# A two-layer graph convolution on one core: blocks of 256 nodes in layer 1, five PSUM banks in layer 2's list

## The chip, the cores and the metric

The kernel runs on one core of a Trainium2 chip. The metric is the time of one execution on the device, in microseconds (us). Before the change it is 3094.66 us, the median of 3 runs (3094.16 to 3096.91). The engines are named as the profile names them: PE (TensorE: matmuls and transposes), DVE (VectorE), ACT (ScalarE), POOL (GpSimd, which issues the gathers) and SP (SyncE, which issues most other transfers).

## The reference, cut to what matters

There are 12500 nodes with 128 features, 200000 edges sorted by their destination, and ten relations. The relation of an edge is the argmax of ten of its 42 attributes.

```python
def _rgcn_layer(x, src, dst, edge_type, w_rel, root, bias):
    N = x.shape[0]
    seg = dst * NUM_REL + edge_type
    xs = x[src]
    sums = jax.ops.segment_sum(xs, seg, num_segments=N * NUM_REL)
    cnt = jax.ops.segment_sum(jnp.ones(seg.shape, x.dtype), seg, num_segments=N * NUM_REL)
    mean = (sums / jnp.maximum(cnt, 1.0)[:, None]).reshape(N, NUM_REL, -1)
    return jnp.einsum('nrd,rdo->no', mean, w_rel) + x @ root + bias
...
edge_type = jnp.argmax(msg[:, NODE_EMB_DIM:-NODE_EMB_DIM], axis=1).astype(jnp.int32)
h = jax.nn.relu(_rgcn_layer(x, src, dst, edge_type, w_rel1, root1, b1))
return _rgcn_layer(h, src, dst, edge_type, w_rel2, root2, b2)
...
x = _layernorm(x + _L0_gnn_ref(...), axis=-1)
```

Each layer gathers the source's row for each edge, averages the rows for each pair of destination and relation, multiplies by the relation's matrix, and adds the node's own row times `root` and a bias. Layer 2 needs `h`, the result of layer 1, of the edge's source, which can be any node.

## The kernel before, in words

**Tiles and bunches.** The edges are cut into 1563 tiles of 128 (`NT`); four tiles (`QB`) are a bunch. For a tile POOL gathers the sources' rows (`gathered`, L747 to 750). DVE writes a one-hot matrix, edge against relation and node, with up to 12 neighbouring nodes (`ones`, L757). ACT scales it by one over the edge's count (`weighted`, L752). PE multiplies the gathered rows by it into a PSUM bank (`zp`, L976 in layer 1, L1479 in layer 2), and DVE adds the product at the tile's place to a ring of 1024 nodes and ten relations in SBUF (`cc`; `sum_into`, L781 to 790). There are two such rings. The order of the instructions on each engine is written out by hand: `layer_1` and `layer_2` are loops over bunches, and the classes `Later` (L792) and its `job` put further work at a tile's number.

**Both layers in one pass.** When all tiles of a block of nodes have been added, `finish` (L838) projects the block. Ten matmuls read the ring, an eleventh adds the `root` part (`projected`, L730, with L737 and L740), ACT evacuates with bias and ReLU (`shifted`, L665), PE turns the block over, ACT copies it (`rows_kept`, L861), and SP stores the rows of `h` to DRAM. They go to `hD` and, for the blocks up to `K1`, to two tables `XH` with rows of 256 numbers: a node's `x` and, once it is ready, its `h` (zero before). From tile 166 (`T0`) on, a gather from `XH` takes both halves, so a tile serves layer 1 and, for sources that are ready, also layer 2: the second matmul of a tile at L976, into the second ring. The block's layer-2 ring is projected in the same way (`second`), and its sum goes to `T2` in DRAM. The rings are then cleared by ACT (`cleared`, L715).

**Epochs.** Which rows of `h` a gather sees must be known when the program is built. The tiles from `T0` on are grouped in 127 rows of 11 tiles (1408 edges). An epoch (L116 to 123) begins with the first row that starts at least `READY` = 6 bunches after a block's `finish`. The gathers of an epoch read one of the two tables, those of the next epoch the other one (`table_of`, L126). A block is stored into the one table as soon as it is ready and into the other one when the epoch that reads that one has ended (`todo_late`, L867 to 873). A table's gather waits for the stores into it, a store waits for the gathers before it.

**The list of layer 2.** Edges whose source was not yet ready, and all edges of the first 166 tiles, are left for `layer_2`. Lines 131 to 181 work out from the share of nodes still missing, with 4.25 deviations of room, how many slots each row needs; in sum 709 tiles of 128 slots (`NT2`). On the chip, `brought_together` (L1057) compacts the 127 rows into this list while the 166 plain tiles are gathered from `hD`: mask (`seen_below`, `rooms`, filled by `row_limits`, L386), prefix sums, a shifting network of eleven steps on DVE, then `listed` (L1218) for the indices, keys, weights and offsets of 128 tiles at a time. `tile_limits` (L404) fills the limits of the offsets.

**Layer 2's loop** (L1450 to 1515) runs over bunches of one or more tiles that fill one PSUM bank. `ones` runs `AH` = 4 bunches ahead of the product, the addition to the ring `BE` = 2 bunches behind it, the products take the three buffers of `ps_y`. Gathers go eight to a buffer, with seven buffers (`GB`). For nodes that spread over more than 48 columns a tile has several bunches, each with its own table of columns (`tables[c, WZ]`, L1169 to 1173, in three banks of PSUM, `mask`). `finish` (L1391) projects a block of 256 nodes, adds `T2`, norms it (`normed`, L691) and stores the output. Its follow-up steps come some tiles later, or at once when all gathers are issued (`u`, L1397).

**Blocks of layer 1.** `starts` (L84): 23 blocks of 512 nodes (`YB`), then six of 128 or less, so 29 calls of `finish`. `KSEEN` = (1, 21) gives 21 epochs.

```python
    starts = list(range(0, N - YB - 2 * P, YB))
    starts += list(range(starts[-1] + YB, N, P))
```

Of the kernel before, what the change touches and what calls it, by code (L numbers as in the profile page):

```python
# [9 lines left out]
F32 = mybir.dt.float32  # L10
# [10 lines left out]
P = 128  # L21
NREL = 10
# [26 lines left out]
KSEEN = (1, 21)  # L49
# [14 lines left out]
def rgcn_resnorm_kernel(ctx: ExitStack, tc: tile.TileContext, x, src, dst, attr, w_rel1, root1, b1,  # L64
# [19 lines left out]
    starts = list(range(0, N - YB - 2 * P, YB))  # L84
    starts += list(range(starts[-1] + YB, N, P))
# [264 lines left out]
    def places():  # L350
# [5 lines left out]
        for size in (YB, P):  # L356
            for k in range(NBLK - 1):
                if done_after(k) < NT and starts[k + 1] - starts[k] == size:
                    early(0, nc.vector.scalar_tensor_tensor(lows, even, STEP * done_after(k) - 0.5, lows,
                                                            op0=ALU.is_gt, op1=ALU.add))  # L360
            if size == YB:
                early(0, nc.vector.tensor_scalar(lows, lows, float(YB // P), None, op0=ALU.mult))
# [310 lines left out]
    def block_rows(a, k, l):  # L673
# [83 lines left out]
    def ones(keys, cols, n, w):  # L757
# [7 lines left out]
        else:  # L765
            nc.vector.tensor_tensor(o.rearrange("p (t r n) -> p t r n", r=NREL, n=w),  # L766
                                    cols[:, None, :, :w].to_broadcast([P, n, NREL, w]),
                                    keys[:, :, None, None].to_broadcast([P, n, NREL, w]), op=ALU.is_equal)
# [61 lines left out]
    def layer_1():  # L830
# [5 lines left out]
        big = [k for k in range(NBLK) if block(k)[1] == YB]  # L836

        def finish(k, t):  # L838
# [22 lines left out]
            def rows_kept(_):  # L861
                pr = po.pop()
                hb = fin.tile([P, 4, C], F32, name="hb")
# [34 lines left out]
            if both:  # L898
                w = 10 if k >= NBLK - 3 else 6
                todo.at(t + w * u, lambda t: cleared(1, k, 0))  # L900
                todo.at(t + (w + 1) * u, lambda t: cleared(1, k, 1))
            if k + 1 < NBLK - 1:
# [16 lines left out]
                w = 2 if k == NBLK - 3 else 5  # L919
# [113 lines left out]
    row_limits()  # L1033
# [23 lines left out]
    def brought_together(ready, first):  # L1057
# [116 lines left out]
        assert WMAX * NREL <= ER  # L1174
# [5 lines left out]
        def put(i, c):  # L1180
# [5 lines left out]
            o = WMAX * NREL + i * (EW // P)  # L1186
# [101 lines left out]
    def layer_2():  # L1288
# [155 lines left out]
        AH, BE = 4, 2  # L1444
# [5 lines left out]
        for p in range(-AH, NB + BE):  # L1450
            if p + AH < NB:
# [3 lines left out]
                ohs[p + AH] = ones(keys[:, t0:t0 + n], tables[(c, WZ) if second else WN], n, w)  # L1455
# [32 lines left out]
            q = p - BE  # L1488
            if q >= 0:
# [199 lines left out]
```

## Time and profile before

| | |
|---|---|
| median of 3 runs | 3094.66 us (3094.16 to 3096.91) |
| profiled execution | 3098.4 us, its span 3096.6 us |
| busy of the span: PE, DVE, ACT, POOL | 78%, 64%, 42%, 75% |
| mean granted PE clock | 0.823 of full speed |
| moved by DMA | 371.57 MB, 120 GB/s in the mean |
| gathers (POOL) | 166 from `x`, 1397 from `XH`, 166 from `hD` for the plain tiles, 709 from `hD` for the list |

How to read it: the span runs from the first to the last instruction of one profiled execution. A line such as `L749 POOL DMA_INDIRECT g<-XH,idxE x1397` is a group: source line, engine, operation, what it writes and reads, and how many. In a timeline each row begins with the start, then the duration; in brackets stands how long the engine had been idle before and what released it. "Issue" is time in which the engine waited for nothing that the profile shows. In a row of stretches each engine has its busy time and its number of instructions, in the order PE, PE's weight loads, DVE, ACT, POOL, followed by the granted clock, the DMA share and GB/s; a row for one engine has that engine's alone. A row of waits has the total, the number and the longest. A group's row by source line has the durations as least/median/greatest in ns and the first and last start in us. Float32 matmuls appear as two records each.

### The profile page before, as it was taken

What the parts mean: (1) busy time and instruction counts of PE and PEld (TensorE: products, weight loads), DVE (VectorE), ACT (ScalarE), POOL (GpSimd) and SP (SyncE); (2) the same over time, 40 slices, a digit from 0 to 9 for tenths busy, and PEclk for the clock granted to TensorE, in tenths of its full rate; (3) what the DMA queues carried; (4) which work ended last, traced back from release to release, by engine and by line L of the source; (5) the groups of instructions that cost most, each with busy time, mean ns of one, the idle gap of its engine ahead of it and who ended that gap; (6) DMA issues with size and microseconds to landing.
All of it is one profiled execution on the core that took longest, in us unless ns stands there. A gap on an engine that the chain in (4) does not pass through costs nothing.

```text
span 3096.6 us, 39943 instructions
## 1 busy us (share of the span) xinstructions
PE 2427.0 (78%) x10905; PEld 1805.4 (58%) x10905; DVE 1989.1 (64%) x5272; ACT 1292.9 (42%) x3006; POOL 2308.9 (75%) x2450
## 2 busy tenths in 40 slices
PE   2768887888888888888888899646577787777887
PEld 2546666566666566666666667545555555555665
DVE  7875746465656565555555554598677677677676
ACT  3543333333333333333333334322445555555453
POOL 7777777777777777777777777677777777777774
PEclk8768888888888878787888789856788999988888
DMA  7865445454545454545454444322222222222222
GB/s 210 233 204 173 143 124 159 120 163 123 163 119 163 121 162 124 162 123 162 123 161 124 127 121 120 101 58 63 60 70 74 73 74 74 74 74 73 74 73 59
DMA packets 260631, 371.57 MB, mean 120 GB/s; under 512 B 49654, under 2 KB 189467, under 8 KB 260404
## 3 DMA queue, kind: packets, MB, share of 16 engines
q0 software_dynamic: 100368, 251.49, 29.5%
q1 hardware_dynamic: 106339, 91.83, 9.6%
q10 hardware_dynamic: 53697, 25.62, 2.8%
q8 instruction: 94, 1.54, 0.2%
q14 instruction: 133, 1.09, 0.1%
HBM read 323.78 MB, written 57.76 MB: 123 GB/s over the span
## 4 chain that ended last, share of the span: by engine, by line
PE 37%; POOL 18%; issue 16%; DVE 13%; DMA 11%; ACT 3%; DVEq 1%; ACTq 0%; POOLq 0%; SPq 0%
POOL g L749 18%; PE pf L737 16%; DMA g<-XH,idxE 10%; PE zp L976 9%; PE zp L1479 8%; DVE cc L790 4%; DVE oh L766 2%; PE pf L740 1%; ACT cc L720 1%; ACT oh L755 1%; DVE cc L1157 1%; PE pf L1195 1%; DVEq L775 1%; DVE oh L763 1%; DVE go L1145 1%
## 5 line engine op out<-in xcount | busy, mean ns | idle before, releaser
L749 POOL DMA_INDIRECT g<-XH,idxE x1397 | 1321.7, 946 | 425.6 <-issue 383.9
L790 DVE TENSOR_TENSOR cc<-cc,zp 128x240 f32 (+16 forms) x2507 | 962.9, 384 | 719.7 <-PE zp L976 503.1
L976 PE MATMUL zp<-oh,g 128*128 128x120 f32 x5920 | 1053.4, 334 | 323.6 <-DMA g<-XH,idxE 230.5
L976 PEld LDWEIGHTS zp<-oh,g 128*128 128x128 f32 x5920 | 926.1, 236 | 482.4 <-issue 187.1
L749 POOL DMA_INDIRECT g<-hD,idxB x709 | 670.2, 945 | 216.1 <-issue 202.7
L755 ACT ACTIVATE oh<-oh,wE 128x120 f32<-128x120 f32 x1729 | 530.2, 383 | 640.8 <-DVE oh L763 557.3
L1479 PE MATMUL zp<-oh,g 128*128 128x120 f32 (+18 forms) x1888 | 514.8, 417 | 256.8 <-DVE cc L790 102.3
L737 PE MATMUL pf<-cc,w 128*128 128x256 f32 (+6 forms) x2120 | 691.4, 485 | 30.3 <-DVE cc L790 21.3
L1479 PEld LDWEIGHTS zp<-oh,g 128*128 128x128 f32 x1888 | 346.1, 230 | 401.8 <-issue 252.2
L737 PEld LDWEIGHTS pf<-cc,w 128*128 128x128 f32 x2120 | 411.8, 208 | 279.6 <-issue 205.0
L755 ACT ACTIVATE oh<-oh,wB 128x150 f32<-128x150 f32 (+18 forms) x778 | 342.6, 483 | 293.7 <-DVE oh L766 276.6
L766 DVE TENSOR_TENSOR oh<-go,keyB 128x480 f32<-128x480 f32 (+14 forms) x478 | 262.9, 550 | 132.8 <-PE zp L1479 131.6
L720 ACT ACTIVATE cc<-zero 128x2560 f32<-128x2560 f32 (+4 forms) x188 | 322.0, 1717 | 21.7 <-DVE cc L790 19.6
L763 DVE TENSOR_TENSOR oh<-bank,keyE 128x480 f32<-128x480 f32 x391 | 253.2, 648 | 0.0
L670 ACT ACTIVATE a<-pf,b 128x512 f32<-128x512 f32 (+1 forms) x27 | 17.3, 639 | 453.6 <-PE pf L740 453.6
L749 POOL DMA_INDIRECT g<-hD,idxE x166 | 158.4, 954 | 62.6 <-issue 46.6
L749 POOL DMA_INDIRECT g<-in_x_dram,idxE x166 | 157.0, 946 | 52.3 <-issue 47.2
L546 DVE TENSOR_TENSOR eqb<-bank,kh 128x1344 bf16<-128x1344 f32 (+2 forms) x65 | 100.5, 1549 | 2.3 <-PE pf L557 1.9
L555 PE MATMUL pf<-eqb,identb 128*128 128x512 bf16 (+2 forms) x130 | 64.7, 498 | 11.6 <-DVE eqb L546 11.4
L882 ACT ACTIVATE v<-pf,b 128x512 f32<-128x512 f32 (+2 forms) x29 | 18.0, 619 | 120.1 <-PE pf L740 100.5
L557 PE MATMUL pf<-eqb,identb 128*128 128x512 bf16 (+2 forms) x130 | 64.1, 493 | 0.0
L415 DVE SCALAR_TENSOR_TENSOR reach<-u,reach 128x6 f32<-128x6 f32 x252 | 42.2, 167 | 7.4
(235 smaller groups left out, 991.5 us busy)
## 6 DMA issues: line engine op xcount, KB each, us to landing
m<-in_edge_attr_dram SPq DMA_DIRECT2D x48, 672.0 KB
g<-XH,idxE POOLq DMA_INDIRECT x1397
XH<-in_x_dram ACTq DMA_DIRECT2D x24, 512.0 KB
XH<-zero ACTq DMA_DIRECT2D x24, 512.0 KB
g<-hD,idxB POOLq DMA_INDIRECT x709
XH<-hb SPq DMA_DIRECT2D x43, 256.0 KB
out_dram<-o SPq DMA_DIRECT2D x47, 128.0 KB
xb<-in_x_dram SPq DMA_DIRECT2D x23, 256.0 KB
```

The lines of the kernel that those rows point to most:

```text
L546: nc.vector.tensor_tensor(eq[:p], kpP[:p, None, :R].to_broadcast([p, DB, R]), fore, op=ALU.is_equal)
L555: nc.tensor.matmul(pc[:p], identb[:p, :p], eq[:p, k:k + 4, L:], start=(d + k == 1), stop=False)
L557: nc.tensor.matmul(pc[:p], identb[:p, :p], back, start=False, stop=(d + k + 3 == L))
L720: nc.scalar.activation(cc[:, l, h * H:(h + 1) * H, o:o + n], zero[:, None, :n].to_broadcast([P, H, n]), AF.Copy)
L737: nc.tensor.matmul(po[:, :n], wsb[l][:, r, :], cc[:, l if ring is None else ring, r, o:o + n], start=(r == 0), stop=False)
L749: nc.gpsimd.indirect_dma_start(out=g[:, j * C:(j + n) * C], out_offset=None, in_=table, in_offset=bass.IndirectOffsetOnAxis(ap=idx, axis=0))
L755: nc.scalar.activation(s, s, AF.Copy, scale=w)
L763: nc.vector.tensor_tensor(o.rearrange("p (t m) -> p t m", m=m), cols[:, None, :m].to_broadcast([P, n, m]), keys[:, :, None].to_broadcast([ ...
L766: nc.vector.tensor_tensor(o.rearrange("p (t r n) -> p t r n", r=NREL, n=w), cols[:, None, :, :w].to_broadcast([P, n, NREL, w]), keys[:, :, ...
L790: nc.vector.tensor_tensor(s, s, z, op=ALU.add)
L976: nc.tensor.matmul(zp[:, a + l * KW:a + (l + 1) * KW], g[:, (slot[j] + l) * C:(slot[j] + l + 1) * C], oh[:, j * KW:(j + 1) * KW], start=Tr ...
L1479: nc.tensor.matmul(zp[:, j * m:(j + 1) * m], gt[:, b * C:(b + 1) * C], oh[:, j * m:(j + 1) * m], start=True, stop=True)
```

## The change

- Layer 1's large blocks have 256 nodes (`BN`), so `finish` is called 52 times. `KSEEN` = (3, 43) covers the same nodes and gives 41 epochs. `hb`, the copy that is stored, has two buffers of half the size; some follow-up steps of `finish` come one bunch sooner.
- `row_limits` is no longer run before layer 1. It is a job from bunch 180 on, one step every two bunches; `tile_limits` moves from bunch 8 to bunch 80.
- The tables `XH` are filled piece by piece in one rhythm (the first piece of the second table comes second), and the last piece at bunch 38 instead of 51.
- Layer 2 keeps one table of 48 columns; for later columns `ones` adds the shift `c` to it. The two banks of `mask` that this frees take products: in five bunches three use `ps_y` and two these banks, once the list is built. From then on additions run three bunches behind (`BE` = 3).

```diff
-KSEEN = (1, 21)
+BN = 2 * P
+KSEEN = (3, 43)
...
-    starts = list(range(0, N - YB - 2 * P, YB))
-    starts += list(range(starts[-1] + YB, N, P))
+    starts = list(range(0, N - YB - 2 * P, BN))
+    starts += list(range(starts[-1] + BN, N, P))
...
-        for size in (YB, P):
+        for size in (BN, P):
...
             was_k, was = starts[k + 1], now
+            yield 1
...
-    def ones(keys, cols, n, w):
+    def ones(keys, cols, n, w, c=0):
...
+            to = o.rearrange("p (t r n) -> p t r n", r=NREL, n=w)
+            a = cols[:, None, :, :w].to_broadcast([P, n, NREL, w])
+            b = keys[:, :, None, None].to_broadcast([P, n, NREL, w])
+            if c:
+                assert n == 1
+                nc.vector.scalar_tensor_tensor(to[:, 0], a[:, 0], float(c), b[:, 0], op0=ALU.add, op1=ALU.is_equal)
+            else:
+                nc.vector.tensor_tensor(to, a, b, op=ALU.is_equal)
...
-                hb = fin.tile([P, 4, C], F32, name="hb")
+                hb = fin.tile([P, 2, C], F32, name=f"hb{k % 2}")
...
-                        assert k <= K0 or t >= first_seen[k - 1]
+                        assert k <= K0 or now + QB >= first_seen[k - 1]
...
-                todo.at(t + (9 if k >= NBLK - 3 else 5) * u, second_kept)
+                todo.at(t + (9 if k >= NBLK - 3 else 4) * u, second_kept)
...
-                w = 10 if k >= NBLK - 3 else 6
+                w = 10 if k >= NBLK - 3 else 5
...
-                w = 2 if k == NBLK - 3 else 5
+                w = 2 if k == NBLK - 3 else 4
...
-        jobs.job(8 * QB, tile_limits(), 2 * QB)
-        for b in range(2):
-            for i, a in enumerate(range(0, N, 2 * YB)):
-                n = i + b * 13
-                jobs.at((1 + n * 3 // 2 if n < 22 else 1 + n * 2) * QB, lambda t, b=b, a=a: table_rows(b, a))
+        jobs.job(80 * QB, tile_limits(), 2 * QB)
+        jobs.job(180 * QB, row_limits(), 2 * QB)
+        pieces = [(b, a) for b in range(2) for a in range(0, N, 2 * YB)]
+        pieces.insert(1, pieces.pop(len(pieces) // 2))
+        for n, (b, a) in enumerate(pieces):
+            jobs.at((1 + n * 3 // 2) * QB, lambda t, b=b, a=a: table_rows(b, a))
...
     places()
-    row_limits()
...
-        for c in range(0, WMAX, WZ):
-            w = min(WZ, WMAX - c)
-            t = mask[:, c * NREL:(c + w) * NREL].bitcast(F32).rearrange("p (r n) -> p r n", n=w)
-            nc.vector.tensor_scalar(t, wide[:, :, :w], float(c), None, op0=ALU.add)
-            tables[c, WZ] = t
+        tables[WZ] = mask[:, :WZ * NREL].bitcast(F32).rearrange("p (r n) -> p r n", n=WZ)
+        nc.vector.tensor_copy(tables[WZ], wide)
...
-        AH, BE = 4, 2
+        AH, BE = 4, 3
+        plain = sum(not b[1] for b in bunches)
...
+            five = p >= plain and "ring" in ready
...
-                zp = zps[p] = ps_y.tile([P, YB], F32, name="zp")
+                if p % 5 > 2 and five:
+                    b = p % 5 - 2
+                    zp = mask[:, b * YB:(b + 1) * YB].bitcast(F32)
+                else:
+                    zp = ps_y.tile([P, YB], F32, name="zp")
+                zps[p] = zp
...
-            q = p - BE
-            if q >= 0:
+            q = p - (BE if five else BE - 1)
+            if q in zps:
```

More of the change, by code (lines that the diff above doesn't have):

```diff
@@ L360, in places @@
                                                             op0=ALU.is_gt, op1=ALU.add))
-            if size == YB:
-                early(0, nc.vector.tensor_scalar(lows, lows, float(YB // P), None, op0=ALU.mult))
+            if size == BN:
+                early(0, nc.vector.tensor_scalar(lows, lows, float(BN // P), None, op0=ALU.mult))
         early(0, nc.vector.tensor_scalar(lows, lows, float(P), None, op0=ALU.mult))
@@ L835, in layer_1 @@
         offs, row = None, None
-        big = [k for k in range(NBLK) if block(k)[1] == YB]
         def finish(k, t):
@@ L859, in rows_out, with rows_kept @@
                 po.append(pr)
-            def rows_kept(_):
+            def rows_kept(now):
                 pr = po.pop()
-                hb = fin.tile([P, 4, C], F32, name="hb")
+                hb = fin.tile([P, 2, C], F32, name=f"hb{k % 2}")
                 for p, s in spans(k):
@@ L1168, in brought_together @@
         yield 1
-        for c in range(0, WMAX, WZ):
-            w = min(WZ, WMAX - c)
-            t = mask[:, c * NREL:(c + w) * NREL].bitcast(F32).rearrange("p (r n) -> p r n", n=w)
-            nc.vector.tensor_scalar(t, wide[:, :, :w], float(c), None, op0=ALU.add)
-            tables[c, WZ] = t
-        assert WMAX * NREL <= ER
+        assert WZ * NREL <= YB
+        tables[WZ] = mask[:, :WZ * NREL].bitcast(F32).rearrange("p (r n) -> p r n", n=WZ)
+        nc.vector.tensor_copy(tables[WZ], wide)
         n = -(-NT2 // P)
@@ L1185, in put @@
             assert m * P <= EW
-            o = WMAX * NREL + i * (EW // P)
+            o = WZ * NREL + i * (EW // P)
             assert o + EW // P <= EW - KW
@@ L1454, in layer_2 @@
                 assert not second or {t0 // P, (t0 + n - 1) // P} <= ready
-                ohs[p + AH] = ones(keys[:, t0:t0 + n], tables[(c, WZ) if second else WN], n, w)
+                ohs[p + AH] = ones(keys[:, t0:t0 + n], tables[WZ if second else WN], n, w, c)
             if 0 <= p + AH - 1 < NB:
```

3 lines of the change are left out of this document (removed).

## The prediction

> **What bounds the kernel now.** The page comes first: the span, the busy times and the chain that ended last.
>
> ```profile
> span 3096.6 us, 39943 instructions
> PE 2427.0 (78%) x10905; PEld 1805.4 (58%) x10905; DVE 1989.1 (64%) x5272; ACT 1292.9 (42%) x3006; POOL 2308.9 (75%) x2450
> PE 37%; POOL 18%; issue 16%; DVE 13%; DMA 11%; ACT 3%; DVEq 1%; ACTq 0%; POOLq 0%; SPq 0%
> ```
>
> Both of the last rows point at PE, with 78% busy and 37% of the chain. That is misleading. A chain followed back from the end can run through PE because PE is waiting for a gather, and a busy share says nothing about who sets the pace. So the second view is the one source line that all of POOL's gathers have (L749): its durations, first and last starts, and what POOL waited for before them.
>
> ```profile
> L749 POOL DMA_INDIRECT g<-XH,idxE x1397: 942/946/1139, 211.8 to 1957.8; - x200
> L749 POOL DMA_INDIRECT g<-hD,idxB x709: 940/944/1436, 2180.1 to 3065.2; - x178
> L749 POOL DMA_INDIRECT g<-in_x_dram,idxE x166: 940/944/1107, 4.1 to 210.5; - x166
> L749 POOL DMA_INDIRECT g<-hD,idxE x166: 940/944/1842, 1971.1 to 2178.8; - x166
>   issue: 680.4, 2233
>   PE zp L976: 28.6, 94
>   DMA hD<-hb: 12.4, 1
> ```
>
> 2233 of the 2438 gathers waited for nothing but their own issue, 0.30 us each. The 94 that stand under PE also waited 0.30 us each (28.6/94), so PE happened to end in that gap and held up nobody. One wait is real, 12.4 us for the last rows of layer 1. The timeline of POOL gives the ends of the two stretches.
>
> ```profile
> 4.15 1.11 POOL L749 DMA_INDIRECT g<-in_x_dram,idxE  x1 [1.98 <-DVE lane L333]
> 1957.81 0.95 POOL L749 DMA_INDIRECT g<-XH,idxE  x1 [0.30 <-issue]
> 1971.11 0.94 POOL L749 DMA_INDIRECT g<-hD,idxE  x1 [12.35 <-DMA hD<-hb]
> 3065.15 0.94 POOL L749 DMA_INDIRECT g<-hD,idxB  x1 [0.30 <-issue]
> ```
>
> Layer 1 has 166+1397 = 1563 gathers, and (1957.81-4.15)/1562 = 1.2507 us from start to start. Layer 2 has 166+709 = 875, and (3065.15-1971.11)/874 = 1.2518 us. A gather with its issue takes 0.945+0.30 = 1.245 us, so POOL loses under 0.01 us per gather in either layer. **POOL's gather rate is the bound everywhere.** The span is 4.15 + 1953.66 + 13.30 (hand-over between the layers) + 1094.04 + 31.45 (last gather's start to the end) = 3096.6 us. The profiled execution took 3098.4 us, 1.8 more than its span, and 3.7 more than the median of the runs, 3094.66.
>
> **The change part by part.** Only what alters the number of gathers, one of the three margins, or POOL's pace can move the time.
>
> *The list of layer 2.* Each row of the list (11 tiles, 1408 edges; 127 rows) keeps the edges whose source lies past the last block of layer 1 that was ready. With blocks of 256 a new limit comes after 2 or 3 rows instead of 5 or 6. Worked through the planner's lines 116 to 181 with both settings, 59 rows have a limit that is 256 nodes higher. That is 256/12500 x 1408 = 28.8 edges fewer in each, 1701 edges or 13.3 tiles of 128. With the allowances and rounding the list falls from 709 tiles (the x709 above) to 695. The plain gathers stay 1563 and 166. So 14 gathers go, 14 x 1.2518 = **-17.5 us**. The count is fixed when the program is built, so no data can take it back.
>
> *Layer 1's finishes, 29 become 52.* PE has 40 us per 256 nodes (32 tiles x 1.25).
>
> ```profile
> 1248.23 8.76 PE L737 MATMUL pf<-cc,w 128*128 128x512 f32 x20
> 2606.46 5.81 PE L737 MATMUL pf<-cc,w 128*128 128x256 f32 x20
> 3040.72 4.48 PE L737 MATMUL pf<-cc,w 128*128 128x256 f32 x20
> 925.81 3.73 PE L976 MATMUL zp<-oh,g 128*128 128x120 f32 x32
> 800.00:1200.00 400.00, 341.21 (x1603) 249.40 (x1601) 233.11 (x530) 153.56 (x364) 302.50 (x321) 0.82 0.48 141
> ```
>
> The tiles' own products take 8 x 16 records x 3.73/32 = 14.9 us of the 40 when PE catches up. The two projections took 8.76 per 256 nodes (half of 2 x 8.76) and will take 2 x 4.48 to 2 x 5.81, so PE needs 23.7 us now and 23.9 to 26.5 then. PE's 341 busy us of 400 become at most 341 + 10 x 2.9 = 370 (10 half-blocks in 400 us): still no bound. PE reaches the gathers' pace again after every finish, and a burst is 5 us long instead of 9. I take **0**. ACT's clears stay the same area, and its evacuations are 23 sets more, beside 153.56 busy of 400.
>
> *Limits and tables on DVE.* `row_limits` had 20 steps of 8 small instructions ahead of layer 1; now 40 steps run from bunch 180 on. `places` gets 23 instructions more.
>
> ```profile
> L383 DVE TENSOR_SCALAR some<-place x86: 83/146/154, 8.9 to 345.3; 128x1 f32<-128x1 f32 x86
> L384 DVE TENSOR_TENSOR rooms<-rooms,some x60: 92/151/221, 10.2 to 84.9; 128x1 f32<-128x1 f32 x60
> L359 DVE SCALAR_TENSOR_TENSOR lows<-even,lows x28: 269/278/280, 44.0 to 54.2; 13x128 f32<-13x128 f32 x28
> 45.00:70.00 25.00, 18.90 (x21) 0.58 0.74 226
> 120.00:145.00 25.00, 18.91 (x21) 0.91 0.60 167
> ```
>
> The old steps (80 pairs of L383 and L384) ran from 9 to 85 us, and POOL's gathers kept their length beside them: 18.90 us for the gathers in 45 to 70 us, 18.91 in 120 to 145 us, after the steps had ended. So the early part loses 160 x 0.15 = 24 us of DVE work and gains 23 x 0.278 = 6.4 us, and neither was on the path. Later, 320 x 0.15 = 48 us lie between tiles 720 and 1040 (about 900 to 1300 us), where DVE has 233 of 400 us busy. **0.**
>
> Here the Trainium skill speaks against the change. Its page "SBUF — State Buffer", section "Who interferes with whom", says that `tensor_scalar` on VectorE can enter a mode that locks GpSimd out of a shared port, and that a DMA issued from GpSimd then waits for its descriptors. By that rule the 80 added L383 instructions could each hold a gather up for their own length, and the sum would be 80 x 0.146 = 11.7 us worse. The two window rows speak against it.
>
> *Layer 1's tables.* The fills of the two tables end at bunch 38 instead of 51.
>
> ```profile
> 160.00:180.00 20.00, 15.12 (x17) 0.50 1.08 344
> 203.81 0.50 SPq L632 DMA_DIRECT2D XH<-hb  x1
> 1232.44 9.32 PE L737 MATMUL pf<-cc,w 128*128 128x512 f32 x20
> 1245.90 0.51 SPq L632 DMA_DIRECT2D XH<-hb  x1
> 1262.09 0.45 SPq L632 DMA_DIRECT2D XH<-hb  x1
> 1277.23 4.98 SPq L459 DMA_DIRECT2D m<-in_edge_attr_dram  x2
> 1954.06 2.75 DMA g<-XH,idxE
> ```
>
> The DMA engines were full at 160 to 180 us (1.08) and POOL still issued 17 gathers per 20 us. The fill now keeps them full for some 20 us longer; the second table is first read at tile 199 (253 us), and its last fill is issued near 190 us. What does add a wait is the change of tables, 41 times instead of 21. A gather that opens an epoch waits for two stores of finished rows, and on POOL every later gather stands behind it. The rows of 1232 to 1262 us are block 14, whose epoch opens at tile 1002, 4.15 + 1002 x 1.2507 = 1257.4 us. Its first store is issued 11.5 us before that, its second one (into the other table) 4.7 us after, when the old epoch's gathers have landed. After the change the same nodes end a block of half the size: the matmuls are some 4 us shorter, so the first store comes about 15 us ahead. The second store's table is needed 33 tiles (41 us) after the epoch opens, in three epochs 22 tiles (27.5 us). Its 4.7 us and a transfer, taken as long as a gather's 2.75, leave 20. If SP is held up by one issue of 4.98 us, both stores still come in time. The tightest opening is the first, at tile 166: the store of 203.81 us stands 8.0 us ahead of the gather at 211.8. The same nodes now end a block of half the size, 4 us sooner, but beside the longer fill. I take **0** for all of this, with 0 to 6 us as bounds, once, for that first opening.
>
> *Layer 2, five banks and additions three bunches behind.*
>
> ```profile
> DVE oh L766 <- PE zp L1479: 131.6, 53, 6.2
> PE zp L1479 <- DVE cc L790: 102.3, 56, 7.7
> L1257 DVE CAST idxB<-pf x6: 221/278/283, 2157.0 to 2291.8; 128x128 int32<-128x128 f32 x5, 128x69 int32<-128x69 f32 x1
> 2000.00:2100.00 100.00, 46.92 (x199) 40.08 (x197) 95.97 (x172) 29.83 (x83) 75.93 (x80) 0.61 0.23 60
> ```
>
> These two waits between PE and DVE will shrink, but POOL, up to 56 tiles (7 buffers of 8) ahead, waited for neither. What is late next is what is late now, the next gather. The list's build is nearly all DVE (95.97 of 100 us); its first indices stand at 2157.3 and POOL reaches them at 2180.1, so 23 us of cover. One copy takes the place of three table additions there. **0**, and a cost only if the build became 23 us longer.
>
> *The end.* This is the one place where three bunches behind can show.
>
> ```profile
> 3073.46 4.88 PE L737 MATMUL pf<-cc,w 128*128 128x280 f32 x20
> 3079.66 0.84 DVE L790 TENSOR_TENSOR cc<-cc,zp 128x240 f32 x2 [5.15 <-PE zp L1479]
> 3080.42 0.60 DVE L698 TENSOR_TENSOR v<-pf,xb 128x256 f32<-128x256 f32 x2
> 3080.55 4.65 PE L737 MATMUL pf<-cc,w 128*128 128x260 f32 x20 [0.60 <-DVE cc L790]
> 3082.67 0.85 DVE L708 TENSOR_SCALAR o<-v,mv,rstd 128x128 f32<-128x128 f32 x3
> ```
>
> Now the last block but one is projected before the last product (3073.46), and the last block 15.4 us after the last gather's start (3080.55). In the new order that block falls due when all gathers are issued, so its norm is written ahead of the last three bunches' additions on DVE. On the same clock: landing 3067.9 (2.75 after the start), product 0.5, projection 4.88 and its closing 0.5, evacuation and transposes 0.9, norm 3.1 (3080.42 to 3083.52), additions 2.1: the last projection starts near 3079.9, 0.7 earlier. Bounds: 6.7 us earlier if nothing but the projection before it held it up (3073.8), 3 us later if PE reaches the end behind. I take **0**, the nearest to 0.7. The 13.30 us between the layers stay, since the last six blocks are the same.
>
> Sum: -17.5 + 0 = 3098.4 - 17.5 = 3080.9 us for a profiled execution, and 3094.66 - 17.5 = **3077.2 us** for the median of runs.
>
> **The rivals.**
>
> *PE becomes the bound in layer 1 (slower).* Against it: 26.5 us of need in 40. It decides from a granted clock below 26.5/40 = 0.66; layer 1 has 0.82 (window row). At 0.61, as in the row of 2000 to 2100 us, a block would take 26.5/0.61 = 43.4 us, 3.4 too many, over 46 blocks 156 us: 3233. The low clock stands where PE has little to do (46.92 busy of 100 us), which speaks against this.
>
> *Gathers wait at the change of tables (slower).* For it: 41 changes at half the distance, and an SP queue that is served in order. Against: the margins above. It decides from 17.5/41 = 0.43 us per change, and from 0.58 us the kernel is slower by more than 0.2%. With stores 1 us too late each time: 3077.2 + 41 = 3118.
>
> *VectorE lengthens the gathers (no change).* 80 more L383, each with at most its own 0.146 us: 3077.2 + 11.7 = 3088.9. Beside the rule of the Trainium skill above nothing is for it, and the window rows are against it.
>
> *The end gives it back.* PE and DVE reach the last gather behind, and the norm delays the additions by more than I reckon: from 11.3 us on the result is within 0.2%. At 12 us, 3089.
>
> That the list doesn't shrink is no rival: its length is fixed.
>
> **How the numbers follow.** A measurement of this kernel can tell 0.2%, 6.2 us, from no change, so faster means below 3088.5. The forecast gets 0.86, PE 0.03, tables 0.05, VectorE 0.02, the end 0.04. Faster 0.86, same 0.06, slower 0.08. The forecast's range is the bounds of the end, 3070.5 to 3080.2, and above them the 6 us of the first change of tables: 3070.5 to 3086.2. It leaves out 0.14, so it needs no reach to the rivals.
>
> **What would show it.** L749 with 695 gathers through idxB; the last gather of layer 1 still near 1958 us, the first through idxB near 2180, the last of all near 3047.6; 31 us after it; 0.30 us before every gather but one. The forecast is wrong if POOL shows waits on XH's stores at first gathers of epochs, if layer 1 ends after 1962 us, if gathers are longer than 0.95 us from 900 to 1300 us, or if the last part exceeds 35 us.

## The result, and the profile after

| | before | after |
|---|---|---|
| median of 5 runs | 3094.66 us | 3215.10 us |
| ratio, 95% interval | | 1.0387 (1.0372 to 1.0403) |
| span of the profiled execution | 3096.6 us | 3211.6 us |
| gathers through `idxB` | 709 | 695 |
| last gather of layer 1, first of the list, last of all | 1957.8, 2180.1, 3065.2 us | 1957.0, 2178.0, 3118.6 us |
| from the last gather's start to the end | 31.45 us | 93.0 us |

The changed kernel is 120 us slower; 3077 were forecast. Some lines stand lower in it: the gathers are L751 (L749 before), the additions L797 (L790), the one-hot builds of the list L775 or, with a shift, L773 (L766), the products of layer 2 L1489 (L1479), the projection L739 (L737), the register loads of the offsets L782 (L775). In the kernels below that are built from the changed one the products of layer 2 stand on lines L1485 to L1498.

The page after, with the span, the busy times and the chain that ended last:

```profile
span 3211.6 us, 42209 instructions
PE 2410.4 (75%) x11861; PEld 1986.2 (62%) x11861; DVE 2037.7 (63%) x5463; ACT 1303.3 (41%) x3177; POOL 2294.2 (71%) x2436
PE 34%; issue 19%; POOL 18%; DVE 15%; DMA 9%; ACT 3%; DVEq 1%; ACTq 0%; POOLq 0%; SPq 0%
```

Nothing here says where 115 us went: PE and POOL were busy 17 and 15 us less than before, DVE 49 us more, in a span that is 115 us longer. The engines wait more. The source line of all gathers shows who makes POOL wait:

```profile
L751 POOL DMA_INDIRECT g<-XH,idxE x1397: 942/946/1060, 211.6 to 1957.0; - x200
L751 POOL DMA_INDIRECT g<-hD,idxB x695: 938/944/1300, 2178.0 to 3118.6; - x174
...
  issue: 677.6, 2224
  PE zp L1489: 53.9, 32
  PE go L1489: 33.6, 19
```

Layer 1 went as forecast: its last gather starts at 1957.0 us and each gather is as long as before. The 51 waits under L1489 are new. They have 87.5 us in all; less the 0.3 us that every gather has, 72 us in which POOL stood still: it had filled its seven gather buffers, and PE had not read them.

The stretches on the two clocks add up. From the start of the first list gather to that of the last: 885.1 us before, 940.6 after, although 14 gathers (17.5 us) are gone: +55.5. The list begins 2.1 us earlier. The end takes 61.5 us more. 55.5 - 2.1 + 61.5 = 115, the difference of the spans. The loss lies in layer 2, in two places: gathers that wait for PE, and a backlog of PE and DVE when the gathers are through.

What PE and DVE wait for is in the rows of waits (total, number, longest). `go` is the name of the large PSUM tile `mask`, in whose second and third bank two of five products now land, and in whose first bank the table stands that the builds read.

```profile
DVE oh L775 <- PE go L1489: 146.3, 115, 6.7
PEld go L1489 <- DVE oh L775: 99.4, 41, 9.5
PE go L1489 <- DVE oh L775: 90.9, 46, 9.3
...
PE zp L1489 <- DVE cc L797: 58.5, 24, 9.2
...
DVE oh L773 <- PE go L1489: 38.8, 26, 6.9
...
DVE oh L775 <- PE zp L1489: 33.6, 9, 6.5
```

In the kernel before, a product hardly ever waited for a build:

```profile
PE zp L1479 <- DVE oh L766: 7.6, 7, 2.7
```

The builds wait for products in that tile, and these products wait for builds. Builds had waited for products before too (131.6 us in 53 waits, 218.7 in 150 by the three rows of builds above); what is new is the other direction, products that wait for builds (90.9 us against 7.6). The timeline shows how it looks (columns: start, duration, instruction, in brackets the idle time before and its end):

```profile
2501.27 0.56 DVE L775 TENSOR_TENSOR oh<-go,keyB 128x400 f32<-128x400 f32 x1
...
2501.89 1.70 PE L1489 MATMUL go<-oh,g 128*128 128x400 f32 x2 [3.73 <-DVE oh L775]
...
2503.38 5.38 PE L739 MATMUL pf<-cc,w 128*128 128x256 f32 x20
...
2503.62 0.57 DVE L775 TENSOR_TENSOR oh<-go,keyB 128x400 f32<-128x400 f32 x1 [1.31 <-PE go L1489]
...
2510.14 0.94 POOL L751 DMA_INDIRECT g<-hD,idxB  x1 [7.12 <-PE zp L1489]
...
2512.32 0.94 PE L1489 MATMUL go<-oh,g 128*128 128x400 f32 x2 [0.79 <-DVE oh L775]
...
2513.37 0.59 DVE L775 TENSOR_TENSOR oh<-go,keyB 128x420 f32<-128x420 f32 x1 [0.62 <-PE go L1489]
```

The one-hot block that a product needs was built four bunches earlier. The build at 2501.27 is for a later product, yet the product at 2501.89 starts when it ends, and the next build (2503.62) starts when that product ends. PE and DVE take turns where they are meant to run side by side, and at 2510.14 POOL has stood for 7 us. For 5.4 of these PE projects a block (2503.38), as it also did in the kernel before; there no gather of the list waited more than 0.3 us for PE.

### The profile page after: what moved, and what is told of

Read it like the earlier page. It is cut to its first block, busy times and chain, and to the rows that moved or that the text cites. A ratio compares the mean times of both kernels' runs of the same rounds, so it can differ in the third digit from the quotient of the medians.

```text
span 3211.6 us, 42209 instructions
## 1 busy us (share of the span) xinstructions
PE 2410.4 (75%) x11861; PEld 1986.2 (62%) x11861; DVE 2037.7 (63%) x5463; ACT 1303.3 (41%) x3177; POOL 2294.2 (71%) x2436
## 4 chain that ended last, share of the span: by engine, by line
PE 34%; issue 19%; POOL 18%; DVE 15%; DMA 9%; ACT 3%; DVEq 1%; ACTq 0%; POOLq 0%; SPq 0%
POOL g L751 18%; PE pf L739 15%; PE zp L983 9%; DMA g<-XH,idxE 7%; DVE cc L797 5%; PE go L1489 5%; DVE oh L775 2%; PE zp L1489 2%; ACT oh L757 1%; PE pf L742 1%; DVE cc L1163 1%; DVEq L782 1%; DVE oh L765 1%; PE pf L1198 1%; DVE st L703 1%
## 5 line engine op out<-in xcount | busy, mean ns | idle before, releaser
L751 POOL DMA_INDIRECT g<-XH,idxE x1397 | 1321.2, 946 | 425.5 <-issue 387.8
L797 DVE TENSOR_TENSOR cc<-cc,zp 128x240 f32 (+11 forms) x2193 | 840.4, 383 | 722.7 <-PE zp L983 395.7
L983 PEld LDWEIGHTS zp<-oh,g 128*128 128x128 f32 x5920 | 876.7, 224 | 477.2 <-issue 182.9
L751 POOL DMA_INDIRECT g<-hD,idxB x695 | 656.3, 944 | 285.5 <-issue 195.4
L739 PE MATMUL pf<-cc,w 128*128 128x256 f32 (+4 forms) x3000 | 749.6, 411 | 48.8 <-DVE cc L797 32.9
L739 PEld LDWEIGHTS pf<-cc,w 128*128 128x128 f32 x3000 | 620.8, 218 | 161.7 <-DVE cc L797 44.4
L757 ACT ACTIVATE oh<-oh,wB 128x150 f32<-128x150 f32 (+23 forms) x771 | 340.7, 483 | 396.0 <-DVE oh L775 308.3
L1489 PE MATMUL zp<-oh,g 128*128 128x120 f32 (+20 forms) x1260 | 326.5, 407 | 106.4 <-DVE cc L797 58.5
L722 ACT ACTIVATE cc<-zero 128x1280 f32<-128x1280 f32 (+3 forms) x274 | 336.7, 1231 | 81.1 <-DVE cc L797 79.7
L1489 PE MATMUL go<-oh,g 128*128 128x160 f32 (+21 forms) x614 | 207.0, 460 | 214.8 <-DVE oh L775 90.9
L775 DVE TENSOR_TENSOR oh<-go,keyB 128x480 f32<-128x480 f32 (+17 forms) x400 | 230.5, 576 | 181.0 <-PE go L1489 146.3
L1489 PEld LDWEIGHTS zp<-oh,g 128*128 128x128 f32 x1260 | 240.2, 236 | 165.0 <-issue 107.6
L1489 PEld LDWEIGHTS go<-oh,g 128*128 128x128 f32 x614 | 116.2, 232 | 292.2 <-ACT oh L757 102.7
L751 POOL DMA_INDIRECT g<-hD,idxE x166 | 158.3, 953 | 61.5 <-issue 46.9
L751 POOL DMA_INDIRECT g<-in_x_dram,idxE x166 | 156.8, 945 | 52.3 <-issue 47.5
L797 DVE TENSOR_TENSOR cc<-cc,go 128x160 f32 (+21 forms) x307 | 119.7, 390 | 38.1 <-PE pf L739 17.2
```

What stands on the lines that cost most here:

```text
L722: nc.scalar.activation(cc[:, l, h * H:(h + 1) * H, o:o + n], zero[:, None, :n].to_broadcast([P, H, n]), AF.Copy)
L739: nc.tensor.matmul(po[:, :n], wsb[l][:, r, :], cc[:, l if ring is None else ring, r, o:o + n], start=(r == 0), stop=False)
L751: nc.gpsimd.indirect_dma_start(out=g[:, j * C:(j + n) * C], out_offset=None, in_=table, in_offset=bass.IndirectOffsetOnAxis(ap=idx, axis=0))
L757: nc.scalar.activation(s, s, AF.Copy, scale=w)
L775: nc.vector.tensor_tensor(to, a, b, op=ALU.is_equal)
L797: nc.vector.tensor_tensor(s, s, z, op=ALU.add)
```

## The experiments

**Theories.** *Shared tile*: the builds' reads of the table and the products in the other banks of the same tile are put in order with one another. Rivals: *additions three behind* hold up the blocks; *contention* of the engines in PSUM; the *blocks of 256* of layer 1 lose the time.

### Which part loses the time

The blocks alone: layer 2's loop, tables and `BE` are those of the kernel before, all else is the changed kernel.

> The blocks of layer 1 from the changed kernel, the layer-2 loop of the kernel before (three tables, products in their own banks only, additions where they were). The same kernel on another chip, where the kernel before itself took 4009 us, told nothing of the bound by the gathers. All three theories that put the loss in layer 2 (shared tile, additions three behind, contention of banks) expect the gain of the 14 shorter tiles alone, 3074 to 3080 us where the kernel before takes 3095, and the last gather about 31 us before the end. A theory that the blocks of 256 lose the time expects over 3150 us.

The layer-2 part alone, in the kernel before:

> The kernel before with layer 2's loop of the changed kernel alone (five buffers, two of them in the tile that holds the table; additions three behind). The three theories that put the loss there expect the whole loss without the gain of the 14 tiles, 3215 to 3240 us, with the waits of the one-hot builds for the products in the shared tile. If the blocks lose the time, it stays within 3090 to 3100 us.

Measured: f1_blocks 3111.66 us (ratio 1.0055, 1.0038 to 1.0072), f2_banks 3235.56 us (1.0455, 1.0438 to 1.0473), beside 3095.13 us for the kernel before on the same chip. So the great loss, 140 us by itself, is layer 2's, within the 3215 to 3240 expected. But no theory had expected f1_blocks: the blocks and the shorter list, for which -17 us had been reckoned, cost 17. That is a second loss, of some 34 us, taken up below.

Then two ways to part the table from the products. In f3 the table goes to SBUF (to make room, two small SBUF tiles of the list's build share places with others):

```diff
-        tables[WZ] = mask[:, :WZ * NREL].bitcast(F32).rearrange("p (r n) -> p r n", n=WZ)
+        cols_w = comp.tile([P, WZ * NREL], F32, name="cols_w")
+        tables[WZ] = cols_w.rearrange("p (r n) -> p r n", n=WZ)
...
```

> The changed kernel with layer 2's table read from SBUF, so that the tile with the two extra products holds nothing else that is read. Shared tile: the waits of the one-hot builds for products in that tile go, and the time falls to 3072 to 3085 us. Additions three behind, or contention of banks: the order and the banks of the products are as they were, so that it stays within 3200 to 3225 us.

In f4 it goes to a PSUM tile of its own, and three products use the old tile:

```diff
+            if five and p5 is None:
+                p5 = p
+                own_bank = ps_y.tile([P, YB], F32, name="zp")
+                to = own_bank[:, :WZ * NREL].rearrange("p (r n) -> p r n", n=WZ)
+                nc.vector.tensor_copy(to, tables[WZ])
+                tables[WZ] = to
...
-                if p % 5 > 2 and five:
-                    b = p % 5 - 2
+                if five and (p - p5) % 5 < 3:
+                    b = (p - p5) % 5
```

> The changed kernel with the table of layer 2 copied to a PSUM tile of its own, the products in three banks of the old tile and two others: still five products in PSUM beside a table in PSUM, additions three behind. Shared tile: 3072 to 3090 us, since no tile is both written by products and read by the one-hot builds. Contention of PSUM reads and writes between the engines, or additions three behind: 3200 to 3225 us as the changed kernel.

f3 took 3120.57 us (1.0088, 1.0071 to 1.0105): 95 us of the loss are gone, though the additions are three behind as before; that is still 36 us above the 3072 to 3085 expected of the shared tile. f4 took 3196.80 us (1.0331, 1.0313 to 1.0348), only 18 less than the changed kernel, a little under the 3200 to 3225 expected of contention or of the additions three behind. The shared tile, in the form in which f4's expectation has it (table against products), fell with this. Its waits on DVE show what had taken the place:

```profile
DVE cc L797 <- PE go L1496: 179.8, 102, 8.2
```

The builds no longer wait for that tile to speak of; the additions do. An addition reads one bank of the tile; the products of up to two later bunches go to its other banks and stand ahead of that addition in the program. With three products in one tile the addition waits for the newest of them. So the theory was widened: whatever reads or writes one tile is kept in order, whichever bank it uses. Contention was still open, since f4 has as much traffic in PSUM as the changed kernel. The test is a kernel in which no two of the six things share a tile (below).

f3 shows something else beside. Its gathers are longer, here as groups of f1_blocks and then of f3 (count, busy us, mean ns, idle before):

```profile
L751 POOL DMA_INDIRECT g<-hD,idxB x695 | 657.0, 945 | 216.5 <-issue 185.9 <-DMA g<-hD,idxB 14.9 <-PE zp L1485 13.5
```

```profile
L751 POOL DMA_INDIRECT g<-hD,idxB x695 | 690.8, 994 | 211.8 <-issue 186.8 <-DMA g<-hD,idxB 14.0 <-PE zp L1490 4.3
```

The mean hides that most gathers are unchanged and some are much longer. The timeline of f3 says which:

```profile
2594.15 0.63 DVE L775 TENSOR_TENSOR oh<-cols_w,keyB 128x450 f32<-128x450 f32 x1 [0.61 <-PE go L1490]
2594.20 1.39 POOL L751 DMA_INDIRECT g<-hD,idxB  x1 [0.30 <-issue]
...
2599.64 0.94 POOL L751 DMA_INDIRECT g<-hD,idxB  x1 [0.30 <-issue]
...
2600.80 0.65 DVE L775 TENSOR_TENSOR oh<-cols_w,keyB 128x480 f32<-128x480 f32 x1
2600.89 1.38 POOL L751 DMA_INDIRECT g<-hD,idxB  x1 [0.30 <-issue]
```

The gathers at 2594.20 and 2600.89 start while a build runs that reads both operands from SBUF, and take 0.44 us longer; the one at 2599.64 starts between builds. Counted over the list, 190 of f3's 695 gathers start during a build and take 1.10 us in the mean (60 of them over 1.2); in f1_blocks 194 do and take 0.94. 690.8 - 657.0 = 33.8 us on the engine that sets the pace: a table in SBUF is no cure. The Trainium skill's page "SBUF — State Buffer", section "Who interferes with whom", says that a VectorE instruction with two SBUF inputs contends with a GpSimd instruction that reads SBUF, and that one with at most one SBUF input, outside its two-port modes, does not. These rows agree, and so do those of f1_blocks, where the table is in PSUM and the gathers keep 945 ns.

### The blocks' own loss: register loads from an odd tile

Before an addition DVE's queue reads where in the ring the tile goes, eight tiles (`GB2`) with one register load. The row by the tile `rowB` has these loads as least/median/greatest in ns; here between 2315 and 2335 us, in the kernel before and in f1_blocks:

```profile
L775 DVEq TENSOR_LOAD <-rowB x3: 595/595/606, 2314.6 to 2334.3; - x3
```

```profile
L782 DVEq TENSOR_LOAD <-rowB x2: 1840/1840/1841, 2316.4 to 2326.0; - x2
```

The same load takes three times as long. The list is cut into two walks, which layer 2 takes in turn; the groups of eight of the second start at its first tile. That was tile 504, a multiple of 8; the blocks of 256 shorten the first walk, and it is 497. The second walk has 198 tiles, 25 loads: 25 x 1.25 = 31 us on DVE. Two kernels test it. One lets the groups of f1_blocks start at multiples of 8:

```diff
-                            m = min(GB2, (UX, NT2)[l] - t)
+                            m = min(GB2 - t % GB2, (UX, NT2)[l] - t)
```

> Blocks of 256 alone, as in f1_blocks (3112 us), and one edit more: the register loads of layer 2's offsets start at multiples of 8 tiles. In f1_blocks the loads of the second walk, which starts at tile 497, take 1.84 us where those of the kernel before, from tile 504, take 0.59. Odd start is the cause: the loads fall to 0.6 us, 25 loads times 1.25 us leave VectorE, and the time falls to 3074 to 3084 us. Rival (the blocks of 256 themselves hold VectorE up, by contention or by the shorter list): the loads or the time stay, 3105 to 3115 us.

> The kernel of g1_aligned once more, for a chip on which the kernel before takes its 3095 us. Odd start of the register loads as the cause of f1_blocks' loss: no load of the second walk over 0.7 us, 3074 to 3084 us. Rival (something else in the blocks of 256): 3105 to 3115 us.

The other puts the odd start into the kernel before:

```diff
-                            m = min(GB2, (UX, NT2)[l] - t)
+                            m = min(GB2 if t != UX else 1, (UX, NT2)[l] - t)
```

> The kernel before with one edit: the second walk's first register load takes one tile, so that the others start at tiles 505, 513 and so on (1 more than a multiple of 8, as 497 is). If the odd start is the cause, these 25 loads take 1.84 us instead of 0.59 and the kernel before becomes slower by up to 30 us: 3105 to 3127 us. Otherwise 3092 to 3098 us.

> The kernel of g4_odd once more: the kernel before with the second walk's register loads at 1 more than multiples of 8 tiles, nothing else. Odd start: these 25 loads take 1.84 us; VectorE is held up by 31 us in all, of which f1_blocks against h1_aligned made 20: 3105 to 3127 us. If the kernel before, with 14 gathers more to hide behind, takes it without loss: 3093 to 3100 us. If the start doesn't matter: loads at 0.6 us and 3093 to 3098 us.

i2_odd took 3116.01 us (1.0062, 1.0045 to 1.0078): +20 us from where the register loads start (and one short load more). 49.6 us follow its last gather instead of 31.45, so most of the loss comes at the end. Its loads and DVE's waits of no visible cause before additions in layer 2 (5.2 us in the kernel before):

```profile
L775 DVEq TENSOR_LOAD <-rowB x2: 1847/1848/1848, 2320.9 to 2332.7; - x2
```

```profile
DVE cc L790 <- issue: 28.5, 26, 1.8
```

h1_aligned took 3091.98 us (0.9980, 0.9971 to 0.9990), 20 less than f1_blocks, with loads of 0.594 to 0.596 us in that stretch (one load, the first of the second walk, takes the seven tiles from 497 and keeps 1.63 us). So the load explains 20 us of some 34, not all: 3074 to 3084 had been expected. Its gathers run without a stop, but 45.1 us follow the last one instead of 31.45:

```profile
L751 POOL DMA_INDIRECT g<-hD,idxB x695: 940/944/1802, 2178.6 to 3046.7; - x174
```

With 14 gathers fewer PE and DVE have 17.5 us less for nearly the same products and additions (1618 matmul records for the list's part against 1632, 808 additions against 816). They arrive late: 44 of these records start after the last gather, 18 in the kernel before, and the end gives 13.6 us back. That they were only a little faster than POOL is the likely reason; i1_own_two, below, takes this backlog away (16 such records).

### Six tiles of their own

The pool of `mask` is opened above `ps_y` (`upper`), and closed once the list is built; three product tiles of their own take its banks. The table stands in a buffer of `ps_y`, as in f4.

```diff
+            if five and ps_t is None:
...
+                upper.close()
+                ps_t = upper.enter_context(tc.tile_pool(name="ps_t", bufs=3, space=PSUM))
...
-                if p % 5 > 2 and five:
-                    b = p % 5 - 2
-                    zp = mask[:, b * YB:(b + 1) * YB].bitcast(F32)
+                if five and (p - p5) % 5 < 3:
+                    zp = ps_t.tile([P, YB], F32, name="zt")
```

> The changed kernel with five products and the table of layer 2 in six PSUM tiles that are their own (the pool of the large tile is closed once the list is made, and another opened in its place). Additions still three behind, table still in PSUM. Shared tile as the cause of the loss: waits of one-hot builds and additions for products of other banks go, 3085 to 3115 us (what f1_blocks takes, with its slow register loads). Contention of banks, or the additions three behind: 3190 to 3220 us, as f4_table_bank and the changed kernel.

> The kernel of g2_own_tiles once more: five products and the table in six tiles of their own, additions three behind, register loads from an odd start. Shared tile as the cause: 3085 to 3115 us. Contention of banks, or the additions three behind: 3190 to 3220 us.

> g2_own_tiles with the register loads at multiples of 8 tiles as well: the change as it could have been. If both causes hold: 3060 to 3080 us, with the last gather about 3048 and 31 us or less behind it. If only the shared tile holds: as g2_own_tiles. If only the loads: 3160 to 3190 us.

> The kernel of g3_own_aligned once more: own tiles and loads from multiples of 8 tiles. Both causes: 3060 to 3080 us. Shared tile alone: as h2_own_tiles. Loads alone: 3160 to 3190 us.

h2_own_tiles took 3089.49 us (0.9980, 0.9970 to 0.9991), beside 3196.80 for f4, which differs in whose tile the three banks are, and in the order in which the two pools are opened. The order between the banks of one tile is the cause; contention and the additions three behind, which both kernels share, are not by themselves. The additions no longer stand among DVE's long waits for these products. What is left are builds that wait for a product, of any tile, as they did in the kernel before (131.6 us there):

```profile
DVE oh L775 <- PE zt L1498: 60.6, 18, 6.9
...
DVE oh L775 <- PE zp L1498: 32.3, 9, 5.1
```

With aligned loads as well, h3_own_aligned took 3084.61 us (0.9964, 0.9950 to 0.9978): faster than before, but over the 3060 to 3080 expected. The last gather stands at 3046.2 us and 39.1 us follow. The timeline of its end:

```profile
3052.35 6.83 PE L739 MATMUL pf<-cc,w 128*128 128x280 f32 x20
...
3063.05 0.84 DVE L710 TENSOR_SCALAR o<-v,mv,rstd 128x128 f32<-128x128 f32 x3
...
3063.82 1.75 DVE L797 TENSOR_TENSOR cc<-cc,zp 128x250 f32 x4
...
3066.19 6.49 PE L739 MATMUL pf<-cc,w 128*128 128x260 f32 x20 [5.44 <-DVE cc L797]
```

The last products were done near 3052.5, but their additions come at 3063.8, after the norm (3063.05) of the block that is projected at 3052.35; and PE waits 5.4 us for them. With additions three bunches behind, the norm is written ahead of them on DVE, and the rows show it running first. One kernel puts the additions two behind again, all else equal:

```diff
-            q = p - (BE if five else BE - 1)
+            q = p - (BE - 1)
```

> h3_own_aligned (3085 us) with the additions of layer 2 two bunches behind, as in the kernel before; five own tiles, the table's own tile and the aligned register loads stay. In h3_own_aligned the last gather starts at 3046.2 us and 39.1 us follow, 31.5 in the kernel before: its last additions stand on VectorE behind the steps that end the block before the last one. If the additions three behind are why, 31 to 33 us follow and the time is 3075 to 3080 us. If five tiles need the third bunch (PE then waits for the additions again, as in h1_aligned): 3085 to 3093 us.

It took 3079.17 us (0.9944, 0.9927 to 0.9961), the fastest of all, and 31.7 us follow its last gather (3045.73), both within what was expected. Most additions now stand ahead of the norm:

```profile
3053.57 6.67 PE L739 MATMUL pf<-cc,w 128*128 128x280 f32 x20 [2.27 <-DVE cc L797]
3053.62 1.84 DVE L797 TENSOR_TENSOR cc<-cc,zp 128x250 f32 x4
...
3061.66 4.64 PE L739 MATMUL pf<-cc,w 128*128 128x260 f32 x20
...
3064.12 0.84 DVE L710 TENSOR_SCALAR o<-v,mv,rstd 128x128 f32<-128x128 f32 x3
```

### The same kernels where transfers are slow

While the runs e1 to e4 and g1 to g4 were made, the kernel before itself took 4009 and 3965 us beside them, on chips 13 and 6; i1 and i2 ran on a chip numbered 6 too, at 3096, so that it isn't known whether the chip or something around it was slow. Their kernels are those of f1 to f4, h1 to h3 and i2.

> The changed layer 1 (blocks of 256, limits late, tables in the new rhythm) with layer 2's loop of before: three product buffers, three tables of columns, additions two bunches behind. If the loss lies wholly in layer 2's new buffers (the shared-tile theory, the three-behind theory and the PSUM-contention theory alike), the 14 gathers that go are worth 17.5 us and the start of the second layer may come 1 to 2 us sooner: 3075 to 3079 us. If the new blocks of layer 1 leave PE behind and that is what layer 2 pays for, it is near 3215 us.

> The kernel before with layer 2's change alone: one table of 48 columns, five product buffers of which two are banks of the tile that holds the table, additions three bunches behind. If layer 2's buffers alone are the loss: 3095 plus about 138 (120 lost in all and 17.5 won by the blocks), 3225 to 3240 us. If the loss needs the blocks of 256: near 3095 us.

> The changed kernel, with the table of 48 columns in SBUF instead of the first bank of the PSUM tile (two small SBUF tiles of the list's build share a place to make room). Five buffers and three behind stay. Shared-tile theory (a product in that tile waits for the one-hot matrix that is built four bunches ahead, since that reads the table, and the next one waits for the product): the waits go, 3075 to 3085 us. Three-behind theory (additions a bunch later hold up the blocks and the end): unchanged, near 3215. PSUM-contention theory (VectorE's reads of the table slow down beside PE's writes): 3075 to 3085 as well.

> The changed kernel, with the table moved to a PSUM bank that is a tile of its own once the list is built; products take the three banks of the old tile and two other buffers. VectorE reads the table from PSUM as before, beside PE's writes to other banks. Shared-tile theory: 3075 to 3090 us. PSUM-contention theory: near 3215. Three-behind theory: near 3215.

All these numbers missed, and so did those of g1 to g4 above, since the bound is another there. Between 400 and 800 us POOL issued 245 gathers in e1_blocks where f1_blocks has 321, of the same length; POOL waited for transfers in between, such as the stores of finished rows:

```profile
POOL g L751 <- DMA XH<-hb: 172.2, 27, 10.4
```

Ratios to the kernel before: e1 1.0099, e2 1.0092, e3 1.0039, e4 1.0212; g1 1.0140, g2 1.0121, g3 1.0083, g4 1.0001. The change of tables, a rival of the prediction, does happen there: 27 such waits with blocks of 256 against 10 in g4, whose blocks are 512, and no kernel with the shorter list is ahead. The order e4 over e3 and g2 over g3 is as at the normal speed; more can't be read from them.

## Why the prediction was wrong, step by step

| median | kernel | step |
|---|---|---|
| 3094.66 | before | |
| 3077.2 | forecast | the list, -17.5 |
| 3079.17 | i1_own_two | the change with every hindrance away |
| 3084.61 | h3_own_aligned | + additions three behind: +5.4 |
| 3089.49 | h2_own_tiles | + odd register loads: +4.9 |
| 3215.10 | after | + products and table in one tile: +125.6 |

The three sizes hold in this order. The two small ones are near the noise: the intervals of neighbouring kernels overlap, though every run of i1_own_two lies below every run of h3_own_aligned. The odd loads cost 20 us where PE and DVE are the ones behind (f1_blocks against h1_aligned), and 5 where five tiles give them room.

- *The list, -17.5*: right. 695 gathers; where nothing holds them up the last one starts at 3045.7 to 3047.0 us (forecast 3047.6). What was missed is that its length sets where the second walk's loads start.
- *Layer 1's finishes, limits, tables: 0*: right at this speed. Layer 1 ended at 1957.0 (forecast 1958), its gathers kept 946 ns, and PE was busy for 326 us of the 400 from 800 us on (341 before, at most 370 reckoned). With slow transfers the tables would not be 0.
- *Layer 2, five banks and additions three bunches behind, 0*: this step failed. It took "these two waits between PE and DVE will shrink" for granted, since two more banks were free. One did: products waited for additions 58.5 us instead of 102.3. The other grew: builds waited for products 218.7 us instead of 131.6. And one that it had not reckoned with came up: products waited 90.9 us and more for builds, 7.6 before. A bank of the same tile is not free of that tile's other users. And "POOL waited for neither" is only true while PE and DVE keep up: once they fell seven gather buffers behind, POOL waited 72 us for them. The prediction itself had asked for 0.30 us before every gather but one, and had named a last part over 35 us as a sign of being wrong; it was 93.
- *The end, 0, bounds -6.7 to +3*: failed too. It was worked out with PE at the gathers' pace. The backlog made it +61.5 in the changed kernel, +13.6 with the blocks alone. Without a backlog, the additions behind the norm cost 5.4 us by the medians (39.1 - 31.7 = 7.4 on the profiled spans), where 0.7 had been reckoned as a gain.
- *Rivals*: "the end gives it back" named the right place for h1_aligned (3091.98, against 3089), not for the change. PE as the bound in layer 1, longer gathers and table changes did not come about. None of them had the tile.
- *What five tiles are worth*: h1_aligned to i1_own_two, 3091.98 to 3079.17, ratio to before 0.9980 to 0.9944. Five banks, put at 0, are a gain of 12.8 us when built with tiles of their own and additions two behind (7.4 with three behind, h3_own_aligned), because they take the backlog away. That i1_own_two lies 2 us from the forecast is therefore in part luck: the forecast gave the list its full 17.5 us without any help of the five banks, and the blocks and the list alone came to 3091.98.

Not settled: whether it is the shape of the load or its start alone that makes an odd register load slow (only starts of 0 and 1 modulo 8 were measured in bulk; one value took 0.31 us in i2_odd, six from tile 689 took 1.42 in f1_blocks, seven from tile 497 took 1.63 in h1_aligned and eight 1.84, which suggests some 0.22 us for each further value of an odd load, an estimate from these four), and whether the chip itself would need any order between two banks of that tile; the kernel without that order was obtained with other tiles, and the wait alone wasn't taken away.

## What to carry to other kernels

Before two engines are given more banks, ask which tile each bank belongs to and who else reads that tile: a free bank of a busy tile is not a free buffer. An engine pair that is only a little faster than the bound is a second bound, and a gain on the bound can be paid back at the end, so the backlog at the last step should be reckoned with the shortened time. And where a list's length changes, look at what is addressed relative to it, down to where a register load starts.

## What the runs showed of the hardware that was not expected

- A register load of eight values took 0.59 to 0.61 us as a rule from tile numbers that are multiples of 8 (single ones up to 1.05), and 1.84 to 2.2 us from 1 above, in f1_blocks, h2_own_tiles and i2_odd, on three chips. The Trainium skill's page "DMA: Bandwidth & Descriptors", section "Latency and other measured facts", gives about 600 ns as the floor of such a load. The aligned loads of eight agree with it, and the odd ones are three times that; but a load of one value took 0.31 us (i2_odd), so 600 ns is no floor here.
- A gather that starts while DVE runs a build with both operands in SBUF took 1.10 us in the mean and up to 1.44, instead of 0.94 (f3_table_sbuf); with one operand in PSUM it stayed at 0.94 (f1_blocks).
- The same kernel took 3965 to 4009 us instead of 3095 where its transfers were slow, and there the question what bounds it has another answer. Why they were slow stays open.
